# Where zeros for S are issued, and when the panels' lists are gathered, in a four-layer graph kernel

## The chip, the cores and the metric

The kernel runs on one core of one Trainium2 chip. The metric is the device time of one execution in microseconds (us); the time of a kernel is the median of its timed runs.

## The reference

Four graph layers are applied one after the other to `x` (32 batch entries, 512 nodes, 256 features, float32), with one adjacency matrix `adj` (512 x 512). An entry of `adj` is nonzero with probability of about 1.6%, and the diagonal always is.

```python
# layers 0 and 3 (h is x; own weights each)
pre_u, pre_v = h @ W1[:256], h @ W1[256:]
S   = sigmoid(relu(pre_u[:, :, None] + pre_v[:, None, :] + b1) @ W2 + b2)  # b, u, v
a_t = einsum('buv,bud->bvd', S * adj, h)
m_t = einsum('uv,bud->bvd', adj, h) * h
h   = beta1 * h + beta2 * (a_t @ Wa + ba) + beta3 * (m_t @ Wm + bm)
# layer 1
z   = h + relu((adj @ h) @ W + b)
# layer 2: attention over the nodes
feats = z @ W1.T ; f1 = feats @ W2 + b2
x   = softmax(leaky_relu(f1[:, None] + f1[None, :]) + adj) @ feats + bias2 + z
```

## The kernel before, in words

`S` is needed only where `adj` is nonzero. The kernel works it out for those places alone and puts the values into an array of zeros in HBM, which it then loads as a dense matrix. (If `adj` has too many nonzeros, another path computes S densely; it doesn't run with these inputs.)

**Groups.** The 32 batch entries go in 8 groups of 4 (`NB`). For each group `first` computes `pre_u` and `pre_v` of layer 0 and writes them to a `table` in HBM (`pre`, L574 to L582; a tile `puv` of 3 buffers, 256 KB for each write by SyncE). One row of the table holds one node's values for the 4 entries (4 KB). `edges` computes S from the table, `middle` does the rest of layer 0, layers 1 and 2, and writes the table of layer 3; `edges` runs again for layer 3, and `last` finishes.

**Items.** `edges` works on 36 items for each group (`ITEMS`). An item is a list of 128 edges, one for each partition. Item (c, k) holds, for each of the 128 rows of chunk c of `adj`, its k-th nonzero off the diagonal (4 chunks, 8 items each, `OWN`). Four further items are the panels: they hold what rows with more than 8 nonzeros have left. For each item GpSimd gathers 128 rows of the table by an index tile `iv` (`fetch`, L607, into `rows` with 5 buffers), VectorE adds the rows of the other end, `mine` (L686), applies relu and W2 (L694 or L702), and the sums go through the sigmoid (L592 to L597), are multiplied by the values of `adj` (L636) and scattered by GpSimd into `cells` in HBM, 16 bytes for each edge (`put`, L601). Scatters to one half of the cells wait for each other. The diagonal, `self_s`, is written by SyncE (L631). Gathers run 3 items ahead, or 5 where spare buffers are named (`rows_more`), which take tiles of the middle stage that aren't in use yet.

**Cells.** There is one pair of cell arrays for layer 0 and one for layer 3, 2 MB an array. Each has to be zero before its first scatter and keeps its zeros afterwards, since the same places are written for each group. A tile `zero` (128 x 1024, filled once by GpSimd) is written to each pair in 8 transfers of 512 KB (`zeros`, L538), for layer 0 in `setup`, for layer 3 in `zeros_behind`, which is listed for a time inside the first group's middle stage. All 16 go through SyncE's queue.

**Building the lists.** `Edges.build` finds the edges, once, on the chip. For each chunk a matmul counts nonzeros along each row (L310, L311); these ranks, with the row of `adj` beside them, are written to `lists` in HBM (L312, 4 transfers of 512 KB). `full` (L313, GpSimd) counts which rows are used up by a panel's line. Then, for the chunks in the order 0, 2, 1, 3, VectorE picks the values of the 8 items (L325) and ScalarE counts their columns (L336), and `slots` makes `iv` and `cell` (L387 to L396). After the four chunks come the panels: small matmuls and VectorE operations give the row of `adj` that each line of a panel belongs to (`node`, `inode`, `iu`; L347 to L362), four gathers bring these rows' lists (`got`, L368, GpSimd), and two VectorE operations for each (L374, L377) pick value and column.

**What sets the order.** Every stage is a generator. `sparse_path` lists the stages with due times in units of one group's middle stage, and `weave` takes their pieces in the order of these times. Each engine's order is then made by a scheduler that may take an instruction ahead of others if nothing keeps it back. `behind` gives an instruction an order (not a wait) after an instruction of a recent piece of the middle stage on its own engine, so that it isn't taken ahead of it. Transfers of zeros had no such order. A queue is worked through in order: an instruction that waits holds up those behind it on its engine. In the built program GpSimd's transfers take eight semaphores in turn, so each waits for the one eight before it.

Of the kernel before, what the change touches and what calls it, by code (L numbers as in the profile page):

```python
# [219 lines left out]
class Edges:  # L220
# [28 lines left out]
    def build(self, counts, adjT, lists, psum, big, tmp):  # L249

        nc, m = self.nc, self.m
        n_small = 1024

        def sheet(n):
            nonlocal n_small
            t = fl[:, n_small : n_small + n]
            n_small += n
            return t

        bf, fl = big(BF16, 4096), big(F32, 2048)  # L260
        upto = bf[:, 0 : NC * N].rearrange("p (c v) -> p c v", c=NC)
        nc.gpsimd.memset(upto, 1.0)
        nc.gpsimd.affine_select(upto, upto, [[-P, NC], [1, N]], ALU.is_ge, 0.0, 0, -1)
        maskT = bf[:, NC * N :].rearrange("p (c v) -> p c v", c=NC)
        before = fl[:, 0:P]
        nc.gpsimd.memset(before, 1.0)
        nc.gpsimd.affine_select(before, before, [[1, P]], ALU.is_gt, 0.0, 0, -1)
        line = fl[:, P : P + LINES]
        nc.gpsimd.iota(line, [[1, LINES]], 0, 0, allow_small_or_imprecise_dtypes=True)
        off = fl[:, 384:512]  # L270
        nc.vector.tensor_scalar(off, m.ident, -1.0, 1.0, ALU.mult, ALU.add)
        ones = fl[:, 512 : 512 + N]
        nc.vector.memset(ones, 1.0)
        step, halfstep = sheet(OWN), sheet(OWN)
        nc.gpsimd.iota(step, [[1, OWN]], 1, 0, allow_small_or_imprecise_dtypes=True)
        nc.vector.tensor_scalar(halfstep, step, -0.5, None, ALU.add)
        row = sheet(NC)
        nc.gpsimd.iota(row, [[0, 2], [P, 2]], 0, 1, allow_small_or_imprecise_dtypes=True)
        nc.vector.tensor_scalar(row, row, float(N), None, ALU.mult)
        spare = sheet(NC * OWN)  # L280
        nc.gpsimd.iota(
            spare, [[0, 2], [OWN * P, 2], [P, OWN]], CELLS, 1, allow_small_or_imprecise_dtypes=True
        )
        rows = []
        for _ in range(2):
            rows.append(big(F32, 2048).rearrange("p (c a v) -> p c a v", c=2, a=2))
        rows = [rows[c // 2][:, c % 2] for c in range(NC)]
        pb = psum()[:, 0:NC]
        base, end = sheet(NC), sheet(NC)
        for c in range(NC):  # L290
            cs, at = slice(c * P, (c + 1) * P), slice(c, c + 1)
            pt = m.adj_turned(c, psum)
            nc.vector.tensor_scalar(maskT[:, c, :], pt, 0.0, None, ALU.not_equal)
            nc.vector.tensor_tensor(maskT[:, c, cs], maskT[:, c, cs], off, ALU.mult)
            nc.scalar.copy(adjT[:, c, :], pt)
            pairs = [(before, counts.lines[:, at])]
            if c % 2:
                pairs.append((ones[:, 0:P], counts.lines[:, c - 1 : c]))
            mm(nc, pb[:, at], pairs)
            nc.gpsimd.tensor_copy(rows[c][:, 1, :], m.adj[:, c, :])  # L300
            nc.gpsimd.tensor_tensor(rows[c][:, 1, cs], rows[c][:, 1, cs], off, ALU.mult)
            yield
        nc.vector.tensor_scalar(base, pb, float(-OWN), None, ALU.add)
        nc.vector.tensor_tensor(end, pb, counts.lines, ALU.add)
        bf2 = big(BF16, 4096)
        full = bf2[:, 0 : NC * LINES].rearrange("p (c s) -> p c s", c=NC)
        for c in (0, 2, 1, 3):
            at = slice(c, c + 1)
            pr = psum()
            mm(nc, pr, [(maskT[:, r, c * P : (c + 1) * P], upto[:, r, :]) for r in range(NC)])  # L310
            nc.vector.tensor_scalar(rows[c][:, 0, :], pr, base[:, at], None, ALU.add)  # L311
            nc.sync.dma_start(lists[c * P : (c + 1) * P, :], rows[c].rearrange("p a v -> p (a v)"))  # L312
            nc.gpsimd.tensor_scalar(full[:, c, :], line, end[:, at], None, ALU.is_ge)  # L313
            yield
        acc, v, there, t = (sheet(NC * OWN) for _ in range(4))
        for c in (0, 2, 1, 3):
            at = slice(c, c + 1)
            js = slice(c * OWN, (c + 1) * OWN)
            target, bias = sheet(OWN), sheet(OWN)
            nc.vector.tensor_scalar(target, step, base[:, at], None, ALU.add)  # L320
            nc.vector.tensor_scalar(bias, halfstep, base[:, at], None, ALU.add)
            for k in range(OWN):
                j = slice(c * OWN + k, c * OWN + k + 1)
                junk = bf2[:, 2048 + k % 2 * N :][:, 0:N]
                nc.vector.scalar_tensor_tensor(  # L325
                    junk,
                    rows[c][:, 0, :],
                    target[:, k : k + 1],
                    rows[c][:, 1, :],
                    ALU.is_equal,  # L330
                    ALU.mult,
                    accum_out=self.value_of(c * OWN + k),
                )

                junk = bf2[:, 3072 + k % 2 * N :][:, 0:N]
                nc.scalar.activation(  # L336
                    junk, rows[c][:, 0, :], AF.Sign, bias=bias[:, k : k + 1], scale=-1.0, accum_out=acc[:, j]
                )
                if k % 2:
                    yield  # L340
            nc.vector.tensor_scalar(v[:, js], acc[:, js], 0.5, float(N // 2), ALU.mult, ALU.add)
            self.slots(js, v, there, t, row[:, at], spare)
            yield

        js = slice(NC * OWN, ITEMS)
        pu = psum()[:, 0 : 2 * PANELS]
        ones_bf = bf2[:, 1024:1025]  # L347
        nc.vector.memset(ones_bf, 1.0)
        for k in range(2 * PANELS):
            h, q = divmod(k, PANELS)  # L350
            mm(nc, pu[:, k : k + 1], [(full[:, h * 2 + c, q * P : (q + 1) * P], ones_bf) for c in range(2)])
        u, node, slot, start, sp, v, there, t = (sheet(2 * PANELS) for _ in range(8))
        nc.vector.tensor_scalar(u, pu, float(HALF - 1), None, ALU.min)
        nc.vector.tensor_copy(node, u)
        nc.vector.tensor_scalar(node[:, PANELS:], u[:, PANELS:], float(HALF), None, ALU.add)
        inode = self.inode
        nc.vector.tensor_copy(inode, node)
        nc.vector.tensor_scalar(self.iu, node, 2.0, None, ALU.mult)
        nc.gpsimd.iota(slot, [[0, 2], [P, PANELS]], 0, 1, allow_small_or_imprecise_dtypes=True)
        nc.vector.tensor_scalar(start, u, float(N), None, ALU.mult)  # L360
        nc.vector.tensor_scalar(sp, slot, float(CELLS + NC // 2 * OWN * P), None, ALU.add)
        nc.vector.tensor_scalar(t, slot, 1.0, None, ALU.add)  # L362
        yield
        gots = []
        for k in range(2 * PANELS):
            gots.append(tmp.tile([P, 2 * N], F32, name=f"got{k}", tag=("h1", "hT1", "mhT0", "hWa0")[k]))
            index = bass.IndirectOffsetOnAxis(ap=inode[:, k : k + 1], axis=0)
            nc.gpsimd.indirect_dma_start(out=gots[k], out_offset=None, in_=lists, in_offset=index)  # L368
        yield
        for k in range(2 * PANELS):  # L370
            at = slice(k, k + 1)
            rank, adj = gots[k][:, 0:N], gots[k][:, N:]
            junk = bf2[:, 2048 + k % 2 * N :][:, 0:N]
            nc.vector.scalar_tensor_tensor(  # L374
                junk, rank, t[:, at], adj, ALU.is_equal, ALU.mult, accum_out=self.value_of(NC * OWN + k)
            )
            nc.vector.scalar_tensor_tensor(junk, rank, slot[:, at], ones, ALU.is_le, ALU.mult, accum_out=v[:, at])  # L377
            yield
        self.slots(js, v, there, t, start, sp, 0)
        yield  # L380

    def slots(self, js, v, there, t, start, spare, off=None):
# [32 lines left out]
class Sparse:  # L415
# [25 lines left out]
    def psum(self):  # L441
        return self.ps.tile([P, N], F32, name="pst", tag="pst")
# [85 lines left out]
            yield  # L528

    def zeros_behind(self):  # L530
        self.zeros(self.cells["3"])
        yield

    def zeros(self, cells):
        for c in cells:
            flat = c[0:CELLS, :].rearrange("(q p a) b -> q p (a b)", q=4, p=P)
            for q in range(4):
                self.nc.sync.dma_start(flat[q], self.zero)  # L538

    def setup_behind(self):  # L540

# [537 lines left out]
def sparse_path(ctx, m, counts, xr, outr, B):  # L1079
# [10 lines left out]
    for t in range(last + 1):  # L1090
# [17 lines left out]
        if t == last:  # L1108
# [2 lines left out]
            behind = end + 0.29, end + 0.45  # L1111
        streams += [
            (sp.first(g0, t * NB), first, "fill"),
            (sp.edges(g0, ("yT", "mhT3") if t == 0 else ()), edges0, ""),
            (sp.middle(g0, g3, t * NB), spread(middle_shares(t == 0), start, end), "main"),
            (sp.edges(g3, ("yT", "h1", "hT1") if t == last else ()), edges3, "free"),
        ]
# [245 lines left out]
```

## Time and profile before

| | |
|---|---|
| timed runs, median of 3 | 3121.13 us (3118.4 to 3138.08) |
| the profiled execution, its own time | 3102.14 us |
| span of the profiled execution | 3100.4 us |
| granted TensorE clock, mean | 0.941 |
| PE, VectorE (DVE), ScalarE (ACT), GpSimd (POOL) busy | 2714.6, 2302.8, 1337.8, 1522.5 us |
| transfers | 679.40 MB, 219 GB/s over the span |
| `cells<-zero`: transfers, size, issue to landing (median) | 16 of 512 KB, 7.3 us |
| `got<-lists`: transfers, issue to landing (median) | 4, 6.2 us |
| `rows<-table`: gathers, issue to landing (median) | 554, 6.1 us |
| `cells<-self_s`: transfers, issue to landing (median) | 32, 6.1 us |

How to read it: the span runs from the first to the last instruction of one profiled execution. Times within it are us from its start. Busy times are averages over stages with different limits; the start, in which the lists are built and nothing of the middle stage can run, has other limits than the rest. In a timeline a row is one or several like instructions of one engine; SPq and POOLq mark the issue of a transfer by SyncE and GpSimd, and "POOL DMA_INDIRECT" is the issue of a gather or scatter.

### The profile page before, as it was taken

Reading aid. Unit: us, or ns where it says so; the run is one execution under the profiler, and the core shown is the slowest. Engines: PE = TensorE matmul, PEld = TensorE weight load, DVE = VectorE, ACT = ScalarE, POOL = GpSimd, SP = SyncE. Lnnn points to the kernel's source line nnn. Section 1 sums busy time; section 2 is a strip of 40 time slices with the busy share of each in tenths; the row PEclk is TensorE's granted clock in tenths of the full one; section 3 lists DMA queues with packets and bytes.
Section 4 is the critical chain, followed back from the end, with each engine's and each line's share of the span. In section 5 each row is a group of like instructions: output and inputs, shape, how many; then the busy total and the mean of one; then the engine's idle time right before and its main releaser. Section 6 shows DMA issues by size and latency. Waiting matters only on the chain.

```text
span 3100.4 us, 32465 instructions
## 1 busy us (share of the span) xinstructions
PE 2714.6 (88%) x8645; PEld 1642.5 (53%) x8646; DVE 2302.8 (74%) x6026; ACT 1337.8 (43%) x4101; POOL 1522.5 (49%) x1312
## 2 busy tenths in 40 slices
PE   6366888889998999989998999989999899889957
PEld 3133444446654565546664565545664566545636
DVE  6783886889589875989589885888679795772761
ACT  3453554445345433545354442545335343453440
POOL 1462453556346563556346562565436563450561
PEclk9688988999999999999999999999999999999978
DMA  8874556786677766786668766787568766551753
GB/s 285 282 236 152 180 174 225 237 268 213 223 224 263 235 210 219 247 282 213 227 213 258 238 197 213 242 267 237 188 216 268 251 221 208 178 174 58 234 195 115
DMA packets 302719, 679.40 MB, mean 219 GB/s; under 512 B 52672, under 2 KB 170944, under 8 KB 294336
## 3 DMA queue, kind: packets, MB, share of 16 engines
q0 software_dynamic: 120384, 406.01, 41.0%
q1 hardware_dynamic: 163184, 234.01, 22.5%
q10 hardware_dynamic: 18960, 37.24, 3.2%
q8 instruction: 70, 1.15, 0.2%
q14 instruction: 121, 0.99, 0.1%
HBM read 531.12 MB, written 146.01 MB: 218 GB/s over the span
## 4 chain that ended last, share of the span: by engine, by line
PE 51%; DVE 18%; DMA 17%; issue 6%; ACT 4%; POOL 3%; SPq 0%; POOLq 0%; ACTq 0%; DVEq 0%
PE pst L45 24%; PE pst L1001 7%; DVE rows L686 6%; DMA table<-puv 5%; DMA rows<-table,iv 5%; PE pst L570 3%; DVE rows L702 3%; PE pst L861 3%; PE pst L1010 3%; PE pst L572 3%; DMA cells<-s,cell 3%; DVE rows L694 3%; PE pst L883 2%; PE pst L840 2%; DMA SA<-cells 2%
## 5 line engine op out<-in xcount | busy, mean ns | idle before, releaser
L601 POOL DMA_INDIRECT cells<-s,cell x576 | 691.1, 1200 | 740.7 <-DMA cells<-s,cell 370.3
L607 POOL DMA_INDIRECT rows<-table,iv x554 | 663.3, 1197 | 672.7 <-DMA table<-puv 148.1
L686 DVE TENSOR_TENSOR rows<-rows,mine 128x1024 f32<-128x1024 f32 x554 | 670.8, 1219 | 164.7 <-DMA rows<-table,iv 148.8
L672 ACT ACTIVATE rows<-rows 128x256 f32<-128x256 f32 x1096 | 442.9, 407 | 516.7 <-DVE rows L694 511.1
L45 PE MATMUL pst<-adj,h 128*128 128x512 f32 x1024 | 451.3, 592 | 0.3 <-PE pst L941 0.3
L702 DVE SCALAR_TENSOR_TENSOR rows<-rows,L_gnn_W2bc 128x256 f32<-128x256 f32 x1120 | 415.9, 419 | 1.8
L45 PE MATMUL pst<-L_gnn_Wa,hT 128*128 128x256 f32 x1024 | 264.3, 410 | 118.6 <-DMA hT<-xT 64.6
L694 DVE SCALAR_TENSOR_TENSOR rows<-rows,L_gnn_W2bc 128x1024 f32<-128x1024 f32 x274 | 332.3, 1216 | 0.3
L45 PEld LDWEIGHTS pst<-adj,h 128*128 128x128 f32 x1024 | 192.8, 190 | 222.4 <-issue 218.4
L45 PEld LDWEIGHTS pst<-L_gnn_Wa,hT 128*128 128x128 f32 x1024 | 207.7, 208 | 165.8 <-issue 53.1
L45 PE MATMUL pst<-eT,feats 128*128 128x512 f32 x512 | 231.5, 606 | 12.4 <-ACT eT L953 12.4
L45 PE MATMUL pst<-adjT,zW 128*128 128x512 f32 x512 | 227.8, 597 | 6.2 <-ACT zW L865 6.2
L1001 PEld LDWEIGHTS pst<-hWa,SA 128*128 128x128 f32 x896 | 213.7, 328 | 7.7 <-issue 4.5
L1001 PE MATMUL pst<-hWa,SA 128*128 128x256 f32 x896 | 216.8, 398 | 0.0
L861 PE MATMUL pst<-WT,hT 128*128 128x256 f32 x512 | 150.3, 459 | 75.9 <-DVE hT L848 75.9
L672 ACT ACTIVATION_READ_ACCUMULATOR rows<-rows 128x1 f32 x1096 | 206.7, 189 | 0.0
L809 ACT COPY flat<-SA 128x512 f32<-128x512 f32 x128 | 137.6, 1128 | 155.0 <-PE pst L45 60.1
L840 PE MATMUL pst<-flat,hWa 128*128 128x512 f32 x448 | 196.8, 592 | 0.0
L861 PEld LDWEIGHTS pst<-WT,hT 128*128 128x128 f32 x512 | 118.0, 235 | 114.9 <-DVE hT L848 88.1
L575 ACT COPY puv<-pst 128x256 f32<-128x256 f32 x256 | 93.7, 370 | 183.8 <-DVE puv L574 168.1
L574 DVE TENSOR_TENSOR puv<-pst,bc_L_gnn_b 128x256 f32<-128x256 f32 x256 | 105.0, 416 | 90.3 <-DMA table<-puv 53.8
L45 PEld LDWEIGHTS pst<-eT,feats 128*128 128x128 f32 x512 | 97.5, 193 | 127.5 <-issue 109.8
(170 smaller groups left out, 3979.3 us busy)
## 6 DMA issues: line engine op xcount, KB each, us to landing
table<-puv SPq DMA_DIRECT2D x256, 256.0 KB, 5.5
SA<-cells POOLq DMA_DIRECT2D x64, 1024.0 KB, 7.0
h<-in_x_dram SPq DMA_DIRECT2D x64, 512.0 KB, 6.4
mine<-table SPq DMA_DIRECT2D x64, 512.0 KB, 5.3
hT<-xT SPq DMA_DIRECT2D x36, 512.0 KB, 5.1
h<-x2s SPq DMA_DIRECT2D x36, 512.0 KB, 4.1
xT<-hT ACTq DMA_DIRECT2D x32, 512.0 KB, 5.5
x2T<-yT SPq DMA_DIRECT2D x32, 512.0 KB, 5.3
```

What stands on the lines that cost most here:

```text
L45: nc.tensor.matmul(out, lhsT, rhs, start=(n == 0), stop=(n == len(pairs) - 1))
L574: nc.vector.tensor_tensor(puv[:, 0, :], pp[:, 0:D], w["b1bc"], ALU.add)
L601: self.nc.gpsimd.indirect_dma_start(out=g.cells[half], out_offset=bass.IndirectOffsetOnAxis(ap=at, axis=0), in_=s, in_offset=None)
L607: self.nc.gpsimd.indirect_dma_start(out=rows, out_offset=None, in_=g.table, in_offset=bass.IndirectOffsetOnAxis(ap=at, axis=0))
L672: self.behind(nc.scalar.activation(part, part, AF.Identity, accum_out=g.s[:, k, b : b + 1]))
L686: self.behind(nc.vector.tensor_tensor(rows, rows, other, ALU.add))
L694: nc.vector.scalar_tensor_tensor(by_entry, by_entry, 0.0, w2, ALU.max, ALU.mult)
L702: nc.vector.scalar_tensor_tensor(part, part, 0.0, w["W2bc"], ALU.max, ALU.mult, accum_out=at)
L809: self.nc.scalar.copy(flat[:, r, :], SA[r][:, :, b])
L840: nc.tensor.matmul(pz, hWa[:, r, cs], flat[:, r, :], start=(r == 0), stop=False)
L861: nc.tensor.matmul(pw[:, at], zT[:, d, cs], m.WT_1[:, d, :], start=(d + k == 0), stop=(d * k == 1))
L1001: nc.tensor.matmul(pz[:, k * D : (k + 1) * D], SA[r][:, cs, b], hWa[:, r, :], start=(r + k == 0), stop=False)
```

## The change

Three things are changed; everything else stays.

1. In `build`, the block that makes `node` and its like and gathers the panels' lists moves from after the four chunks to the middle of their loop, ahead of the third chunk (c = 1). The lists are gathered into other tiles: one tile for two of them with the tag `eT`, and those with the tags `h1` and `hT1`, where before it was `h1`, `hT1`, `mhT0` and `hWa0`. The operations that use the lists (L374, L377) stay at the end. The first group's `edges` takes `yT`, `mhT0` and `hWa0` as spare row buffers, where it took `yT` and `mhT3`.
2. `zeros` issues its 8 transfers from GpSimd's queue.
3. `zeros_behind` fills the tile `zero` again, with a VectorE memset that is ordered behind the middle stage. The zeros of layer 3 read that tile, so they wait for the memset.

```diff
         for c in (0, 2, 1, 3):
+            if c == 1:
+                pu = psum()[:, 0 : 2 * PANELS]
...
+                yield
+                gots = []
+                two = tmp.tile([P, 2, 2 * N], F32, name="got", tag="eT")
+                for k in range(2 * PANELS):
+                    if k < 2:
+                        gots.append(two[:, k, :])
+                    else:
+                        gots.append(tmp.tile([P, 2 * N], F32, name=f"got{k}", tag=("h1", "hT1")[k - 2]))
+                    index = bass.IndirectOffsetOnAxis(ap=inode[:, k : k + 1], axis=0)
+                    nc.gpsimd.indirect_dma_start(out=gots[k], out_offset=None, in_=lists, in_offset=index)
+                yield
             at = slice(c, c + 1)
...
-        gots = []
-        for k in range(2 * PANELS):
-            gots.append(tmp.tile([P, 2 * N], F32, name=f"got{k}", tag=("h1", "hT1", "mhT0", "hWa0")[k]))
-            index = bass.IndirectOffsetOnAxis(ap=inode[:, k : k + 1], axis=0)
-            nc.gpsimd.indirect_dma_start(out=gots[k], out_offset=None, in_=lists, in_offset=index)
-        yield
         for k in range(2 * PANELS):
...
     def zeros_behind(self):
+        self.behind(self.nc.vector.memset(self.zero, 0.0))
         self.zeros(self.cells["3"])
         yield
...
             for q in range(4):
-                self.nc.sync.dma_start(flat[q], self.zero)
+                self.nc.gpsimd.dma_start(flat[q], self.zero)
...
-            (sp.edges(g0, ("yT", "mhT3") if t == 0 else ()), edges0, ""),
+            (sp.edges(g0, ("yT", "mhT0", "hWa0") if t == 0 else ()), edges0, ""),
```

As built, GpSimd's order becomes: the eight zeros of layer 0, then the four L313; the first `got`, four gathers of `rows`, the other three `got`, four more gathers, and from there gathers and scatters as before. The eight zeros of layer 3 stand in the first group's middle stage, after the twelfth gather for the second group and ahead of that group's first scatter; their memset stands on VectorE between the L596 and L597 of that group's first four items.

More of the change, by code (lines that the diff above doesn't have):

```diff
@@ L316, in build @@
         for c in (0, 2, 1, 3):
+            if c == 1:
+                pu = psum()[:, 0 : 2 * PANELS]
+                ones_bf = bf2[:, 1024:1025]
+                nc.vector.memset(ones_bf, 1.0)
+                for k in range(2 * PANELS):
+                    h, q = divmod(k, PANELS)
+                    mm(nc, pu[:, k : k + 1], [(full[:, h * 2 + c, q * P : (q + 1) * P], ones_bf) for c in range(2)])
+                u, node, slot, start, sp, vp, therep, tp = (sheet(2 * PANELS) for _ in range(8))
+                nc.vector.tensor_scalar(u, pu, float(HALF - 1), None, ALU.min)
+                nc.vector.tensor_copy(node, u)
+                nc.vector.tensor_scalar(node[:, PANELS:], u[:, PANELS:], float(HALF), None, ALU.add)
+                inode = self.inode
+                nc.vector.tensor_copy(inode, node)
+                nc.vector.tensor_scalar(self.iu, node, 2.0, None, ALU.mult)
+                nc.gpsimd.iota(slot, [[0, 2], [P, PANELS]], 0, 1, allow_small_or_imprecise_dtypes=True)
+                nc.vector.tensor_scalar(start, u, float(N), None, ALU.mult)
+                nc.vector.tensor_scalar(sp, slot, float(CELLS + NC // 2 * OWN * P), None, ALU.add)
+                nc.vector.tensor_scalar(tp, slot, 1.0, None, ALU.add)
+                yield
+                gots = []
+                two = tmp.tile([P, 2, 2 * N], F32, name="got", tag="eT")
+                for k in range(2 * PANELS):
+                    if k < 2:
[5 more added lines that the diff above has]
+                yield
             at = slice(c, c + 1)
@@ L343, in build @@
             yield
[L345 to L348, printed above, removed]
-        for k in range(2 * PANELS):
[L350 to L362, printed above, removed]
-        yield
-        gots = []
-        for k in range(2 * PANELS):
-            gots.append(tmp.tile([P, 2 * N], F32, name=f"got{k}", tag=("h1", "hT1", "mhT0", "hWa0")[k]))
-            index = bass.IndirectOffsetOnAxis(ap=inode[:, k : k + 1], axis=0)
-            nc.gpsimd.indirect_dma_start(out=gots[k], out_offset=None, in_=lists, in_offset=index)
-        yield
         for k in range(2 * PANELS):
@@ L374, in build @@
             nc.vector.scalar_tensor_tensor(
-                junk, rank, t[:, at], adj, ALU.is_equal, ALU.mult, accum_out=self.value_of(NC * OWN + k)
+                junk, rank, tp[:, at], adj, ALU.is_equal, ALU.mult, accum_out=self.value_of(NC * OWN + k)
             )
-            nc.vector.scalar_tensor_tensor(junk, rank, slot[:, at], ones, ALU.is_le, ALU.mult, accum_out=v[:, at])
+            nc.vector.scalar_tensor_tensor(junk, rank, slot[:, at], ones, ALU.is_le, ALU.mult, accum_out=vp[:, at])
             yield
-        self.slots(js, v, there, t, start, sp, 0)
+        self.slots(slice(NC * OWN, ITEMS), vp, therep, tp, start, sp, 0)
         yield
```

## The prediction

> **What bounds the kernel now.** I read the page first, for the whole span.
>
> ```profile
> span 3100.4 us, 32465 instructions
> ...
> PE 2714.6 (88%) x8645; PEld 1642.5 (53%) x8646; DVE 2302.8 (74%) x6026; ACT 1337.8 (43%) x4101; POOL 1522.5 (49%) x1312
> ...
> DMA  8874556786677766786668766787568766551753
> ...
> PE 51%; DVE 18%; DMA 17%; issue 6%; ACT 4%; POOL 3%; SPq 0%; POOLq 0%; ACTq 0%; DVEq 0%
> ```
>
> Over the span TensorE is the bound, with VectorE in the chain. The first slices (77.5 us each) differ: the transfers are 8, 8 and 7 tenths busy there while PE stands at 6, 3, 6. On every engine the changed kernel's instructions stand in the same order as before from the second batch entry's softmax (355 us here) to the end, so what the change does is done in the first 360 us or so. There I read the chain of waits, then the queues.
>
> ```profile
> 38.14 7.20 DMA table<-puv
> ...
> 66.44 7.62 DMA table<-puv
> ...
> 78.62 4.52 DMA mine<-table
> ...
> 103.15 12.24 DMA cells<-self_s
> ...
> 138.15 4.26 DMA got<-lists,inode
> ...
> 268.22 7.49 PE pst L840 x10
> ```
>
> Start, duration, what: the chain of the start runs over transfers, and the middle stage's first sums (L840) begin at 268.2 us. SyncE's queue says why the transfers are late:
>
> ```profile
> 23.86 12.93 SPq L538 DMA_DIRECT2D cells<-zero  x8
> 38.14 0.61 SPq L582 DMA_DIRECT2D table<-puv  x1
> ...
> 87.20 3.95 SPq L538 DMA_DIRECT2D cells<-zero  x5
> 103.15 0.94 SPq L631 DMA_DIRECT2D cells<-self_s  x2
> ```
>
> The eight zero transfers of layer 0 hold SyncE for 12.9 us (1.6 us each; one `h` load takes 0.4), and the first `table` write and all `lists` writes stand behind them. The eight of layer 3, which nothing needs before the last stage, were pulled to 64.6 to 91.2 us: three between `table` writes, five just ahead of the diagonal `self_s`. Two waits and the transfers' rate complete it:
>
> ```profile
> POOL rows L607 <- DMA mine<-table: 52.8, 1, 52.8
> DVE big L374 <- DMA got<-lists,inode: 16.0, 1, 16.0
> ```
>
> ```profile
> 90.00:100.00 10.00, 1.86 (x8) 1.78 (x8) 8.85 (x10) 5.27 (x23) 4.52 (x4) 0.50 1.02 394
> 130.00:140.00 10.00, 0.00 (x0) 0.00 (x0) 0.00 (x0) 0.00 (x0) 6.46 (x7) 0.50 0.37 111
> ```
>
> Columns of the second: window, then busy us of PE, PE's loads, DVE, ACT, POOL, clock, share and GB/s of the transfers. At 90 us the transfers are full (394 GB/s); at 130 us everything but GpSimd stands still, because VectorE waits (126.5 to 142.4 us) for `got`, and `got` stands on GpSimd's queue behind scatters that wait for each other.
>
> **What the Trainium skill says.** "DMA: Bandwidth & Descriptors", section "Issuing engines are not separate DMA queues": transfers of SyncE, ScalarE and GpSimd run on the same 16 engines and interleave; another issuer saves issue time only. The trace agrees on the sharing: 364 to 401 GB/s from 30 to 50 us is one total. But here the issue time is the matter (12.9 us on SyncE). Same page, "Queues, rings and completion order": an engine takes turns between queues that have work, and takes each queue's descriptors in order. So zeros on GpSimd's queue no longer stand before `table`, but stand before any gather issued after them; no run here shows the turns. "SBUF — State Buffer", section "SBUF: two separate sides": some VectorE operations lock GpSimd out of writing descriptors. The gathers' 0.94 to 2.0 us fit that, without proving it.
>
> **The change, part by part.** Durations are of the profiled execution: span 3100.4 us, 3102.14 us with what lies around it; the three timed runs have a median of 3121.13, 19 us more, so I work out a difference and take it off the median.
>
> (a) Zeros of layer 0 leave SyncE. Eight issues go before GpSimd's four L313; GpSimd's plain transfers take about 0.58 us each (the two L727 at 262.1 take 1.15), so 5 us, and L313 (26.2 to 30.3 us) ends near 33. Its user, the four small matmuls for `node`, comes well after 40 us: nothing. The 4.19 MB still move. Gained: the stalls of VectorE and ScalarE behind `table` (4.5 us at 41, 3.3 us at 70), the `h` load that PE awaits for 6.2 us at 44, and ScalarE's 6.5 us at 28.7, spent in its own issues. These overlap. Two bounds: VectorE is busy 48.8 us between 20 us and its first gathered rows, so the first gather can't start before about 71; and 20 to 83 us move some 21.7 MB, less 1.6 MB for three zeros of layer 3, which at 380 GB/s take 53 us, so 73. I take 74 for 83.1: **-9 us** (-5 to -13).
>
> (b) Zeros of layer 3 leave the start. From the first gather, the first rows reach VectorE after 6.9 us (90.0); I take the median landing of 6.1, so 80. VectorE then works 13 us, nearly without a gap, to `self_s` (103.15), so 93. `self_s` landed after 12.2 us, behind 2.6 MB of zeros; the median of its 32 transfers is 6.1, so 99 instead of 115.4. That is 16 us in all, **-7** of them here (-3 to -10).
>
> (c) The lists' gathers leave the scatters. In the built order the first `got` stands ahead of the first gathered rows, three more after four rows, where GpSimd would soon wait for free buffers. The 16 us that VectorE waits are not all won: from 143 to 225 us GpSimd issues one transfer after another with gaps of 0.3 us, so GpSimd sets the rate, and what leaves its path is four issues of 0.96 us with gaps of 0.3: **-5 us** (-16 if VectorE sets the rate). Late next: the first scatters to one half, which wait for each other (116.2, 122.4, 126.5, 131.7); they stay. The third spare row buffer lets one more gather go early; nothing to a microsecond. VectorE has less time per item before the first scatter: it had worked 26 us from its first row by then, and would have 20, so I give back **+2** (0 to 5). `h1` and `hT1`, which hold the last two lists, come free with the last panel, as before.
>
> The start's sum: -9 - 7 - 5 + 2 = **-19 us** at L840.
>
> (d) Zeros of layer 3 in the middle stage. A new memset on VectorE (0.95 us, by GpSimd's own at 13.5 us) stands between L596 and the reciprocal at 330.1 us, and the eight transfers wait for it, on GpSimd, right after the gather at 329.3:
>
> ```profile
> 329.30 1.68 POOL L607 DMA_INDIRECT rows<-table,iv  x1 [0.84 <-DVE rows L702]
> 331.29 1.00 POOL L601 DMA_INDIRECT cells<-s,cell  x1 [0.30 <-issue]
> 332.59 0.95 POOL L607 DMA_INDIRECT rows<-table,iv  x1 [0.30 <-issue]
> ...
> 344.25 1.22 DVE L686 TENSOR_TENSOR rows<-rows,mine 128x1024 f32<-128x1024 f32 x1
> ```
>
> Behind them are the scatter of 331.3 and the gather of 332.6, whose rows VectorE takes at 344.25 (counted by buffers). Eight issues of 0.58 us move them to 336 and 337.3, and 4.19 MB go first: 10.5 us at 400 GB/s, 15 at 285. The rows then land at about 347 (to 352), VectorE is due at 345.2 with the memset, so it waits 2 us (0 to 8), and TensorE after it, since this is the softmax stretch whose chain is on VectorE and ScalarE. The scatters, each waiting for the one before, fall 13 us behind; GpSimd's idle 6 us at 355 and 9 us at 372 take that up, and their results are read at 457. Price: 0.95 + 2, rounded up for the next rows: **+4 us** (+1 to +9).
>
> Sum: -19 + 4 = **-15 us**: 3106 us, and about 3087 for a profiled execution.
>
> **Rivals.** *The wait goes whole* (0.15): VectorE, not GpSimd, sets the rate after 126 us, so its 16 us count (11 more), and (a) reaches its bound of 13 (4 more): -30, so 3091. For it: PE, DVE and ACT are all idle from 130 to 140. Against: GpSimd's unbroken issues after.
> *The start is bound by its bytes* (0.17): layer 0's zeros take a share of full transfers wherever they come from, so (a) is -3, (b) -4, (c) -5, +2, and (d) +4: -6, so 3115. For it: 364 to 401 GB/s from 30 to 50. Against: SyncE's 12.9 us with `table` waiting.
> *Slower* (0.10): the zeros clog GpSimd's queue at 331 us. If they get half of the page's mean of 219 GB/s, 4.19 MB take 38 us instead of 12, the rows for 344 us land near 372, VectorE and TensorE wait some 27 us, and 19 won become 8 lost: 3129. It decides once the zeros need more than about 31 us, that is under 135 GB/s. For it: gathers and scatters share that one queue (q0 is 41% of the transfers' time). Against: 394 GB/s were reached at 90 us by nearly the same mix.
>
> **How the numbers follow.** My forecast has 0.58, its own range is -25 to -5: 3096 to 3116. To leave no more than 2 in 10 out, the range reaches to the rivals, 3088 to 3126. A measurement of this kernel can tell about 1% (31 us) from no change. Faster by that needs the whole-wait rival and a little more, or the forecast's own bounds: 0.14. Slower needs the clog at well over its price: 0.05. The rest, 0.81, lies within.
>
> **What would show it.** Right: the first gathered rows are issued near 74 us, `self_s` lands near 99, `got` is waited for less than 2 us, L840 starts near 249 and VectorE waits 2 to 4 us some 14 us after the memset. (a) is wrong if the first gather is still past 79; (b) if `self_s` takes over 9 us; (c) if L840 is earlier by 16 us more than the landing of `self_s` is; (d) if no wait for rows follows the memset, or one over 10 us. The whole is wrong if L840 is less than 8 us or more than 30 us earlier.

## The result, and the profile after

| | before | after |
|---|---|---|
| median | 3129.84 us | 3117.05 us |
| lowest to highest | 3116.01 to 3138.08 us | 3106.34 to 3141.21 us |
| ratio, 95% interval | | 0.9966 (0.9954 to 0.9979) |

By the ratio the change saves 10.6 us of 3130 (6.6 to 14.4 by the interval; the two medians are 12.8 apart). Timed a second time the ratio was 0.9975 (0.9960 to 0.9991), 7.8 us. The forecast was 15 us off a median of 3121.13, 3106 us. That median came from the first three of the twenty runs of before that are in this table, so the ratio is the better measure. The kernel became faster, as forecast, by 0.7 and 0.5 of the 15 us in the two timings. But the gain is put together otherwise than was forecast: the zeros brought little, and the lists more (see below).

The page of the profile after, its span and busy times:

```profile
span 3112.8 us, 32475 instructions
...
PE 2713.5 (87%) x8645; PEld 1639.7 (53%) x8646; DVE 2302.9 (74%) x6027; ACT 1337.7 (43%) x4101; POOL 1531.2 (49%) x1328
```

This span is 12 us longer than that of before although the kernel is faster. So the two spans can't be subtracted: single executions of one kernel lie some 35 us apart, and both profiled executions of the kernel before (there is a second below) lie at the low end of its times. What can be read are marks early in the span, where the change works, and only beside their own scatter. The chain of waits of the profile after reaches back over the last few per cent of the span alone, so the start is read from the timeline. SyncE's queue first:

```profile
29.06 0.60 SPq L587 DMA_DIRECT2D table<-puv  x1
...
42.48 2.30 SPq L587 DMA_DIRECT2D table<-puv  x2
...
103.30 0.91 SPq L636 DMA_DIRECT2D cells<-self_s  x2
```

The 12.9 us of zeros are gone and the first `table` write is out at 29.06 in place of 38.14. But the second one is not out before 42.48 (it was 39.99). What SyncE waited for between them stands in its waits (first line: us in total, times, longest), and why it was late in the list of transfers from 20 to 60 us (count, size, median us from issue to landing):

```profile
SPq L587 <- DMA L_gnn_Wa<-in_L_gnn_Wa_dram: 9.4, 1, 9.4
```

```profile
cells<-zero POOLq DMA_DIRECT2D x8, 512.0 KB, 11.9
...
L_gnn_Wa<-in_L_gnn_Wa_dram ACTq DMA_DIRECT2D x1, 256.0 KB, 12.8
```

SyncE's and ScalarE's transfers share eight semaphores in the built program. A weight load of 256 KB that ScalarE issued at 29.55 landed only after 12.8 us, among GpSimd's zeros, and SyncE's next write had to wait for it. So SyncE is still held up, now between two `table` writes. GpSimd's timeline:

```profile
22.91 4.40 POOL L543 DMA_DIRECT2D cells<-zero  x8
...
75.36 1.36 POOL L345 DMA_INDIRECT got<-lists,inode  x1 [44.19 <-DVE inode L330]
80.00 0.98 POOL L612 DMA_INDIRECT rows<-table,iv  x1 [3.27 <-issue]
...
111.85 1.01 POOL L606 DMA_INDIRECT cells<-s,cell  x1 [11.80 <-DVE rows_more L691]
```

First gathered rows at 80.00 (83.13 before), first scatter at 111.85 (116.20). In the windows of before, VectorE had 0.00 us busy from 130 to 140; now:

```profile
90.00:100.00 10.00, 0.39 (x2) 0.39 (x3) 9.58 (x15) 6.12 (x29) 8.28 (x6) 0.50 1.03 411
...
130.00:140.00 10.00, 0.00 (x0) 0.00 (x0) 10.00 (x24) 4.45 (x21) 8.17 (x7) 0.50 0.67 189
```

VectorE is busy for nearly the whole of both windows, and `got` is no longer in its list of waits. TensorE's second burst of first sums, and then the middle stage, on GpSimd and on VectorE:

```profile
255.15 6.06 PE L845 MATMUL pst<-flat,big 128*128 128x512 f32 x10 [12.58 <-ACT flat L814]
```

```profile
317.30 4.32 POOL L543 DMA_DIRECT2D cells<-zero  x8 [0.63 <-DVE s L602]
```

```profile
316.09 0.91 DVE L535 MEMSET zero<- 128x1024 f32 x1 [0.15 <-issue]
...
334.16 1.22 DVE L691 TENSOR_TENSOR rows<-rows,mine 128x1024 f32<-128x1024 f32 x1 [3.31 <-DMA rows<-table,iv]
```

The sums start 13.1 us earlier than in the profile of before. Eighteen us after the memset VectorE has waited 3.3 us for rows, which were gathered behind the zeros.

### The profile page after: what moved, and what is told of

The parts are those of the page before. It is cut to its first block, busy times and chain, and to the rows that moved or that the text cites. A ratio compares the mean times of both kernels' runs of the same rounds, so it can differ in the third digit from the quotient of the medians.

```text
span 3112.8 us, 32475 instructions
## 1 busy us (share of the span) xinstructions
PE 2713.5 (87%) x8645; PEld 1639.7 (53%) x8646; DVE 2302.9 (74%) x6027; ACT 1337.7 (43%) x4101; POOL 1531.2 (49%) x1328
## 5 line engine op out<-in xcount | busy, mean ns | idle before, releaser
L866 PEld LDWEIGHTS pst<-WT,hT 128*128 128x128 f32 x512 | 121.4, 242 | 136.6 <-DVE hT L853 107.1
L579 DVE TENSOR_TENSOR puv<-pst,bc_L_gnn_b 128x256 f32<-128x256 f32 x256 | 104.4, 414 | 95.8 <-DMA table<-puv 58.6
```

The costliest lines, as they stand in the source:

```text
L579: nc.vector.tensor_tensor(puv[:, 0, :], pp[:, 0:D], w["b1bc"], ALU.add)
L866: nc.tensor.matmul(pw[:, at], zT[:, d, cs], m.WT_1[:, d, :], start=(d + k == 0), stop=(d * k == 1))
```

## The experiments

All times below are marks of one profiled execution each, in us from the start of its span, beside the timed ratio to the kernel before. "Sums" is the start of the second burst of first sums, "2nd" and "4th" are the second and fourth store of `x2T` by SyncE, that is, two points further on in the first group's middle stage.

| kernel | first rows | first scatter | sums | 2nd | 4th | ratio (95%) |
|---|---|---|---|---|---|---|
| before | 83.1 | 116.2 | 268.2 | 369.4 | 478.4 | |
| before_again | 80.6 | 111.9 | 266.0 | 366.2 | 472.3 | |
| after | 80.0 | 111.9 | 255.2 | 359.9 | 468.4 | 0.9966 (0.9954 to 0.9979) |
| after_again | 78.5 | 111.7 | 261.1 | 365.6 | 475.3 | 0.9975 (0.9960 to 0.9991) |
| lists_only | 81.9 | 109.0 | 255.1 | 355.9 | 465.1 | 0.9945 (0.9922 to 0.9969) |
| lists_only_2 | 80.6 | 105.7 | 254.3 | 353.5 | 462.6 | 0.9952 (0.9938 to 0.9966) |
| zeros_only | 79.0 | 112.8 | 265.6 | 370.2 | 478.2 | 0.9987 (0.9971 to 1.0003) |
| zeros3_early | 86.4 | 118.8 | 262.7 | 362.3 | 467.4 | 1.0003 (0.9984 to 1.0022) |
| zeros3_spread | 77.8 | 109.5 | 253.3 | 354.7 | 463.9 | 0.9956 (0.9941 to 0.9970) |
| zeros3_sync | 79.4 | 110.5 | 254.9 | 361.8 | 471.2 | 0.9972 (0.9957 to 0.9987) |
| zeros0_late | 77.6 | 111.1 | 255.4 | 362.6 | 468.7 | 0.9953 (0.9939 to 0.9968) |
| lists_spread | 81.5 | 107.4 | 255.6 | 359.8 | 466.0 | 0.9948 (0.9933 to 0.9964) |
| late_spread | 77.9 | 111.3 | 255.5 | 358.1 | 463.2 | 0.9965 (0.9944 to 0.9986) |
| more_gathers | 82.6 | 113.6 | 264.9 | 369.8 | 478.4 | 0.9986 (0.9970 to 1.0002) |
| zeros_more | 90.8 | 124.4 | 270.0 | 375.6 | 485.3 | 0.9994 (0.9979 to 1.0009) |

**The two kernels once more** (no edit).

> The changed kernel once more, for its marks in a second profile: first gathered rows issued at 80, first scatter at 112, the middle stage's first sums (second burst) at 255, fourth store of x2T at 468 us (before: 83, 116, 268, 478), and some 0.3% (10 us) under the kernel before. If the profile of before was only a lucky execution in its later part, the marks up to 500 us come again within 2 us and the span of this profile differs freely.

> The kernel before once more, for the scatter of its marks: first gathered rows 83, first scatter 116, first sums 268, fourth x2T store 478 us. If the first profile was a lucky execution only in its later part, these come within 3 us, and from the eighth to the sixteenth store takes some 710 us as in the other kernels' profiles, where the first profile had 700.

Of one and the same program the marks came up to 6 us apart (sums of the changed kernel 255.2 and 261.1, fourth store 478.4 and 472.3 before), so the 2 and 3 us of the expectations were too tight, and only means or differences over several kernels say something below 5 us. On means: first rows 81.9 before and 79.3 after, first scatter 114.1 and 111.8, sums 267.1 and 258.1, 2nd store 367.8 and 362.7. The stretch from the eighth to the sixteenth store took 700 and 702 us in the two profiles of before, and 706 to 717 in all others. In the built program nothing differs there and the timed runs say the opposite, so I put it down to these executions, without having shown what makes it.

**Each part alone.** `lists_only` takes the lists' part and leaves the zeros as before; `zeros_only` the reverse:

```diff
 lists_only (against after)
-        self.behind(self.nc.vector.memset(self.zero, 0.0))
         self.zeros(self.cells["3"])
...
-                self.nc.gpsimd.dma_start(flat[q], self.zero)
+                self.nc.sync.dma_start(flat[q], self.zero)
 zeros_only (against before)
+        self.behind(self.nc.vector.memset(self.zero, 0.0))
         self.zeros(self.cells["3"])
...
-                self.nc.sync.dma_start(flat[q], self.zero)
+                self.nc.gpsimd.dma_start(flat[q], self.zero)
```

> Only the lists' part of the change; all zeros stay on SyncE, without the memset. If the early lists carry the gain (theory): VectorE no longer waits for `got`, the first sums start some 9 us earlier than before (259), nothing is lost in the middle stage, so the fourth x2T store is near 469 and the time 8 to 10 us under before: as good as the whole change. If the zeros carry it (rival): first sums 263 to 264, the fourth store near 474, 4 us under before. If the parts only work together (rival): no change.

> Only the zeros' part: all on GpSimd's queue, those of layer 3 behind the memset; the lists are gathered late as before. Theory: first gathered rows near 80, first scatter near 112, but the wait for `got` of some 16 us is there, so the first sums come 3 to 5 us earlier than before (264) and the zeros in the middle stage take 5 us back: fourth store at 478, time equal to before within 3 us. Rival (the zeros carry the gain): first sums near 259, fourth store at 474, 5 us or more under before.

> The early lists alone, a second time, since the first was timed in seven runs only. If it is better than the whole change by what its zeros cost in the middle stage (about 4 us), it is again 14 to 18 us under before, ratio 0.9945 to 0.9955; first sums at 253 to 258, first sums to second x2T store 100 to 102. If the first was luck: 0.9965 to 0.9975 like the whole change.

The lists alone are worth 15 to 17 us, more than expected (8 to 10), and the zeros alone 4 (-1 to 9). The lists carry the gain, and with the zeros added it is smaller by the ratios (0.9966 and 0.9975), though the intervals overlap. SyncE's queue with the lists alone suggests why the zeros of layer 3, five of them behind the first gathers, hurt little there:

```profile
81.70 1.38 SPq L635 DMA_DIRECT2D cells<-self_s  x2
...
100.34 13.07 SPq L542 DMA_DIRECT2D cells<-zero  x5
```

In this program's order `self_s` stands 21 us earlier than in the changed kernel (103.30), ahead of the five zeros. So it isn't late for the first scatter, and the five zeros go out from 100 to 113 us, where VectorE waits for no transfer. The edit changes the built order as well as the queue, so what sets this kernel apart from the changed one isn't the price of the zeros alone. With the zeros alone, VectorE's wait for the lists is there, 10.7 us long.

**What the lists' gathers cost where they stood.** Four gathers of the same number of rows are put back on GpSimd into the scatter stretch, and nobody waits for them:

```diff
+        more = tmp.tile([P, 2 * N], F32, name="more", tag="mhT3")
+        quarters = lists.rearrange("n (a v) -> (n a) v", a=4)
+        for k in range(2 * PANELS):
+            index = bass.IndirectOffsetOnAxis(ap=self.iv[:, 3 * OWN + k : 3 * OWN + k + 1], axis=0)
+            out = more[:, k * N // 2 : (k + 1) * N // 2]
+            nc.gpsimd.indirect_dma_start(out=out, out_offset=None, in_=quarters, in_offset=index)
```

> The changed kernel with four more gathers of 128 rows on GpSimd in the scatter stretch, about where the lists' gathers stood before (after some eight scatters); their data, a quarter as wide, go into a tile that nothing reads. They put back the issue time that the change took off GpSimd's path there, 4 x 0.96 us and four gaps of 0.3, 5 us, and no wait of VectorE. If GpSimd sets the rate of that stretch (the step of the prediction), the first sums come 5 us later than with the changed kernel: 260 against 255 in the first profile, 266 against 261 in the second. If VectorE sets it (theory, after the lists alone gained 13 us there), 0 to 2 us later, and the time stays 0.2 to 0.4% under before.

```profile
143.56 1.14 POOL L379 DMA_INDIRECT more<-lists,iv  x1 [0.30 <-issue]
145.00 1.83 POOL L379 DMA_INDIRECT more<-lists,iv  x1 [0.30 <-issue]
147.14 1.51 POOL L379 DMA_INDIRECT more<-lists,iv  x1 [0.30 <-issue]
148.95 0.95 POOL L379 DMA_INDIRECT more<-lists,iv  x1 [0.30 <-DMA more<-lists,iv]
150.21 1.37 POOL L618 DMA_INDIRECT rows<-table,iv  x1 [0.30 <-ACT puv L586]
```

Here the theory that I had written down (VectorE sets the rate) fell and the step of the prediction stood. From the first scatter to the sums it takes 152.0, 154.0 and 152.8 us in the three profiles with late lists (mean 152.9) and 143.3 to 149.3 in the eleven with early lists and no extra gathers (mean 145.6). The four extra gathers, 6.65 us of GpSimd from 143.56 to 150.21, bring it to 151.3: 5.7 of the 7.3 us are back, though VectorE waits for nothing there (10.00 of 10 us busy in each window from 110 to 150). This is one profile, and the eleven spread over 6 us, so the 5.7 is known to some 2 us; the time agrees (0.9986 against 0.9966 and 0.9975). So GpSimd's issues lie on the path of the scatters. They aren't all of it: in the kernel before GpSimd also waits for earlier scatters to land, between 105 and 250 us:

```profile
POOL cells L601 <- DMA cells<-s,cell: 18.7, 9, 5.0
```

VectorE's wait for `got` was mostly slack, not the price: it was 16.0, 13.6 and 10.7 us in the three profiles with late lists, and the stretch of 152 to 154 us doesn't follow it. The third spare row buffer, which belongs to the lists' part, wasn't tried apart.

**The zeros of layer 3.** `zeros3_early` leaves them on SyncE without the memset (in the built order all eight then stand ahead of `self_s`); `zeros3_sync` sends them from SyncE behind the memset; `zeros3_spread` one at a time from GpSimd:

```diff
 zeros3_spread (against after)
         self.behind(self.nc.vector.memset(self.zero, 0.0))
-        self.zeros(self.cells["3"])
-        yield
+        for c in self.cells["3"]:
+            flat = c[0:CELLS, :].rearrange("(q p a) b -> q p (a b)", q=4, p=P)
+            for q in range(4):
+                self.behind(self.nc.gpsimd.dma_start(flat[q], self.zero))
+                yield
...
-        (sp.zeros_behind(), spread(even(2), 0.15, 0.2), ""),
+        (sp.zeros_behind(), spread(even(9), 0.15, 0.45), ""),
```

> The changed kernel, but layer 3's eight zeros stay on SyncE without the memset; in the built order all eight stand ahead of self_s. Theory: self_s lands later again (12 us or more), the first scatter is at 115 to 117 and the first sums near 259 to 260; in the middle stage VectorE's wait of 3.3 us for rows and the memset are gone, so the fourth store is near 468 to 470, the same as with the whole change: moving these zeros gained as much in the start as it cost later. Rival (the wait in the middle is hidden): the fourth store is at 473 or later. Rival (their bytes in the start cost nothing): first sums at 255 and the fourth store near 463.

> The changed kernel, but layer 3's eight zeros go out of SyncE's queue, still behind the memset, and stand after the second group's self_s there. If only the order on GpSimd's queue sets the price, first sums to second x2T store is 101 to 102. If bytes and a held queue count wherever they are (theory), the rows are late again or layer 3's table writes stand behind the zeros on SyncE: 103 to 106.

> The changed kernel, but layer 3's eight zeros are issued one at a time between the gathers and scatters of the middle stage, all behind the memset. So far the way from the first sums to the second x2T store took 104.5 to 104.7 us in the three profiles with the eight zeros in one block there, and 99.6 to 101.2 in the three without. Theory (the price is the rows standing behind 4 MB on GpSimd's queue): 101 to 102, VectorE's 3 us wait for rows gone, 2 to 3 us better than the whole change in total. Rival (the price is the bytes, or the memset's place): 104 to 105 as before, and nothing won.

From the sums to the 2nd store the five profiles without zeros in that stretch took 101.2, 100.3, 100.8, 99.2 and 99.6 (mean 100.2). With the block of eight on GpSimd it took 104.5 to 104.9 in four profiles and 105.6 and 107.1 in two: the block costs 4.4 us in the changed kernel and 5 over all. Spread, it took 101.4 here (102.6 and 104.2 in the two kernels below), about half, and VectorE's wait for rows is gone from its list. From SyncE it took 106.9, no better; VectorE waits as long for its rows, and the load of `mine` at 327.4 us stands behind the eight on SyncE:

```profile
DVE rows L691 <- DMA rows<-table,iv: 4.5, 1, 4.5
```

So the price is not a matter of GpSimd's queue alone: in these two kernels 4 MB in one go delay the rows from either queue. In the start the eight cost more (`zeros3_early`): first rows at 86.4 against 79.3 with the changed kernel, and 1.0003 in time, so nothing of the lists' gain is left. The expectation that moving them gains as much as it costs is refuted by the timing; its marks from the sums on (262.7, fourth store 467.4) would have fitted it. Where this kernel loses its time after the fourth store isn't shown.

**Layer 0's zeros later.** They wait for chunk 0's columns:

```diff
-        self.zeros(self.cells["0"])
         yield
-        for _ in range(NC + 2 * (OWN // 2 + 1)):
+        for k in range(NC + 2 * (OWN // 2 + 1)):
             next(edges)
+            if k == NC + OWN // 2:
+                self.nc.gpsimd.tensor_scalar(self.zero[:, 0:1], self.e.found, 0.0, None, ALU.mult)
+                self.zeros(self.cells["0"])
             yield
```

(`found` is the first column of `v`, as chunk 0's `slots` leaves it.)

> The changed kernel, but layer 0's zeros wait on GpSimd for the columns of chunk 0 (about 57 us, by a small operation of 128x1 that GpSimd puts ahead of them) in place of going out at 23 us. Theory (the start up to 60 us is bound by its bytes, so it did not matter which queue sent them): weights, lists and table land earlier, the first gathered rows are issued at 73 to 76 (changed kernel: 80.0 and 78.5), and the first sums come 3 to 5 us earlier. Rival (VectorE's work ahead of the index of the panels sets the first gather): 78 to 80 as before. Rival (the zeros now meet the lists and the first rows): first gather before 77 but first rows late by as much, no gain at the first sums.

Windows of this kernel, columns as above (the third busy time is VectorE):

```profile
30.00:40.00 10.00, 10.00 (x36) 4.90 (x35) 9.44 (x31) 3.48 (x10) 0.00 (x0) 1.00 0.92 325
40.00:50.00 10.00, 8.68 (x27) 4.27 (x26) 8.30 (x34) 7.84 (x22) 2.51 (x4) 1.00 1.02 359
50.00:60.00 10.00, 6.92 (x19) 2.72 (x18) 4.80 (x18) 5.02 (x14) 2.63 (x6) 0.84 1.03 404
60.00:70.00 10.00, 8.73 (x24) 3.99 (x25) 5.68 (x26) 2.54 (x7) 0.00 (x0) 0.65 0.92 332
```

From 30 to 50 us VectorE works 17.7 of 20 us where the changed kernel has 11.3 (6.23 and 5.05), and from 50 to 70, after the zeros went out at 48.1, only 10.5 where that has 18.1. The stall went with the zeros, and the first rows still stand at 77.6, where the five profiles with the changed kernel's start have 77.8 to 82.6. SyncE's wait for ScalarE's weight load was down from 9.4 to 2.0 us here, so that wait by itself doesn't set the first gather. In time the kernel was 0.9953, a little better than the changed one, but the intervals overlap.

**More zeros.** Layer 3's zeros are sent once more from GpSimd in the start, after L313:

```diff
-        for _ in range(NC + 2 * (OWN // 2 + 1)):
+        for k in range(NC + 2 * (OWN // 2 + 1)):
             next(edges)
+            if k == NC - 1:
+                self.zeros(self.cells["3"])
             yield
```

> The changed kernel with eight more zero transfers (layer 3's cells, once more than needed) on GpSimd's queue in the start, right behind the four L313, where GpSimd has nothing else to do. No other engine issues anything for them and no instruction reads what they write before the stage much later, so what they cost is their 4.19 MB alone. If the stretch up to the first gather is bound by its bytes (theory: that is why it did not matter which queue layer 0's zeros came from), 4.19 MB at some 390 GB/s are 10.7 us, less what the emptier stretch from 60 to 80 us takes up (0.22 of 20 us, 4): the index of the panels and the first gathered rows come 6 to 11 us later, rows at 85 to 90. If VectorE's own work and the order on the engines bind it (rival), 0 to 2 us later.

```profile
89.21 1.33 POOL L345 DMA_INDIRECT got<-lists,inode  x1 [44.43 <-DMA table<-puv]
90.84 0.98 POOL L614 DMA_INDIRECT rows<-table,iv  x1 [0.30 <-issue]
```

First rows at 90.8: 11.6 us later than the mean of the changed kernel, the whole 4.19 MB at 361 GB/s and nothing taken up by the emptier stretch, as far as a mark that scatters by some 2 us tells. VectorE's waits for `table` from 28 to 92 us rose from 11.0 to 22.2. All 11 us arrive at the sums (270.0 against 258.1). So bytes sent while the transfers are full (410, 406 and 412 GB/s from 30 to 60 us here) count one for one. Those sent later don't: `lists_only` and its repeat send three zeros of layer 3, 1.6 MB, from 60.7 to 71.6 us, `lists_spread` below sends none before 300 us, and the first rows stand at 81.9, 80.6 and 81.5.

**Two combinations.** `lists_spread` is `zeros3_spread` with layer 0's zeros on SyncE; `late_spread` is `zeros0_late` with the zeros of layer 3 spread.

> The early lists, layer 0's zeros on SyncE as before, and layer 3's zeros one at a time in the middle stage from GpSimd behind the memset. In the built order self_s stands early on SyncE, as with the lists alone (there issued at 81.7 us, with the changed kernel at 103.3). Theory: first scatter at 105 to 109, first sums at 252 to 255, first sums to second store 101 to 102, fourth store at 463 to 466, 16 to 20 us under before: the best of all. Rival (five of layer 3's zeros stood behind self_s anyway and cost nothing): no better than the lists alone; worse by 1 to 3 us if the spread zeros still hold up rows.

> The changed kernel with both: layer 0's zeros held back until chunk 0's columns are found, and layer 3's zeros one at a time in the middle stage. Theory (their gains add): first rows to VectorE at 84 to 86, first sums at 252 to 255, 101 to 102 us from there to the second x2T store, fourth store at 462 to 466 and 0.5 to 0.6% under before, as good as the lists alone. Rival (both run into the same limit): no better than either by itself, 0.45%.

Neither is better than the lists alone: 0.9948 and 0.9965, and the gains do not add. The best versions are `lists_only` (0.9945 and 0.9952, median 3096.7 us in its longer timing against 3113.9 of before) and `lists_spread` (0.9948), which can't be told apart. Both beat the kernel before; the lists alone are also ahead of the changed kernel, by some 4 to 9 us by the ratios, though the intervals of their second timings overlap (0.9938 to 0.9966 and 0.9960 to 0.9991). A start without layer 0's zeros at all wasn't tried, since the cells would then hold no defined values.

## Why the prediction was right and wrong, step by step

**(a) Layer 0's zeros off SyncE: -9 forecast, -2.6 measured** (first rows, means of two profiles each; against 83.1 the first profile alone gives -3.1). Without the lists' part it is the same (`zeros_only`, 79.0), so the first `got` ahead of the rows doesn't hold them up. This step failed, and so did (b): they missed by 6 and 7 us. By the prediction's own sign, the first gather was past 79 in one profile and just under in the other. The small parts were right: eight issues took 4.4 us, and L313 ended at 31 at no cost. What failed first is the gain that was counted on, VectorE's stalls behind `table`. They didn't go, they grew (28 to 92 us, before and after; 6.7 and 10.5 in the second profiles):

```profile
DVE puv L574 <- DMA table<-puv: 7.8, 2, 4.5
DVE puv L579 <- DMA table<-puv: 11.0, 6, 4.9
```

What failed next is "two bounds, I take 74": VectorE's work (71) and the bytes (73) were set side by side as if the larger one held. (By the trace they were also too high: VectorE is busy 48.1 us from 20 to 83.1, and the transfers move 317 GB/s there, 20.0 MB and not 21.7; that gives 68 for either.) In the run they follow one another in part. The windows of the changed kernel, columns as above:

```profile
30.00:40.00 10.00, 5.92 (x24) 2.83 (x22) 6.23 (x20) 0.90 (x4) 1.18 (x3) 0.99 1.04 409
40.00:50.00 10.00, 9.44 (x17) 3.93 (x18) 5.05 (x17) 4.17 (x12) 0.00 (x0) 0.67 0.99 362
...
60.00:70.00 10.00, 8.88 (x28) 4.29 (x27) 9.44 (x42) 7.01 (x20) 0.00 (x0) 1.00 0.78 266
70.00:80.00 10.00, 9.37 (x39) 4.70 (x38) 8.89 (x36) 7.23 (x21) 1.36 (x1) 1.00 0.78 252
```

From 30 to 50 us, while the zeros fill the transfers, `table` writes and weight loads are late and VectorE works 11.3 of 20 us; from 60 to 80 it works 18.3 and the transfers aren't full. Before, it was 15.1 and 14.6. (The second profiles have 16.5 and 16.8 before, 11.5 and 18.7 after.) The change moved VectorE's stall forward and did not remove it. `zeros0_late` turns the two halves round and gains 2 us at most at that point; `zeros_more` adds bytes to the full stretch and pays for them in full. The rival "bound by its bytes" had -3 here, and its mechanism is what the runs show for the full stretch. The sentence of the Trainium skill that the prediction set aside here ("DMA: Bandwidth & Descriptors", "Issuing engines are not separate DMA queues": another issuer saves issue time only) fits the -2.6 us better. SyncE's waits of the kernel before, from 23 to 37.5 us, already say so:

```profile
SPq L538 <- DMA xT<-hT: 3.5, 1, 3.5
SPq L538 <- DMA bc_L_gnn_beta<-in_L_gnn_beta_dram: 2.2, 1, 2.2
SPq L538 <- DMA col_L_gnn_b<-in_L_gnn_b_dram: 1.7, 1, 1.7
SPq L538 <- DMA big<-in_L_gnn_ba_dram: 1.2, 1, 1.2
SPq L538 <- DMA L_gnn_Wm<-in_L_gnn_Wm_dram: 0.4, 1, 0.4
```

9.0 of the 12.9 us in which the zeros held SyncE were waits for other transfers to land, ScalarE's above all. I had taken them for issue time. When the zeros were gone, SyncE waited 9.4 us for a landing instead.

**(b) Layer 3's zeros out of the start: -7 forecast, nothing or next to it at the first scatter** (-2.3 in all there, where (a) alone makes -2.6). The landing was right: `self_s` took 7.7 us in place of 12.2, under the 9 of its sign. It was issued at 103.30 all the same, because the terms ahead of it were too small: rows came to VectorE 7.9 us after the first gather and not 6.1, and VectorE needed 15.5 us to `self_s` and not 13, with picks of chunk 3 and `puv` work between the items. So 111 and not 99. The lists' gathers, which now stand among those of the rows, aren't the reason: in `zeros_only`, without them, VectorE needed 18.8 us there (85.6 to 104.4).

**(c) The lists off the scatters' path: -5 + 2 = -3 forecast, -7.3 measured.** The mechanism is right and shown: GpSimd's issues are on the path, VectorE's 16 us are not what counts, and four issues put back cost 5.7 of the 7.3 us. The reading behind it was too neat: of GpSimd's gaps between 143 and 225 us seven are longer than 0.3 us, 11.6 us in all. The mis-sized term is the give-back of 2 for VectorE, of which nothing is seen. `got` is not waited for at all (the sign was under 2 us). The sign against (c), that the sums gain 16 us more than the landing of `self_s`, didn't come.

**(d) Layer 3's zeros in the middle: +4 forecast, +4.4 measured** in the changed kernel, 5 over all kernels with the block. The memset took 0.91 us (0.95), the wait came 18 us after it (14) and was 3.3 and 4.4 us (2, bounds 0 to 8). GpSimd's queue did not clog: the eight landed after 6.9 us in the median, where the slower rival needed some 31 us for all of them.

**The sum.** At the sums -19 was forecast; the two pairs of profiles give -13.1 and -4.9, on means -9.0. With (d) that leaves -4.6 at the 2nd store (-5.1 read off), while the timed runs say -10.6 and -7.8. The difference is within what these marks scatter; I can't say more on it. That the total came as near as it did is in part luck: the zeros' parts of the start missed by some 14 us, and the lists' part made up for 4 of them. The range of 3088 to 3126 and the 1% bound held.

## What to carry to other kernels

Where transfers are full first and an engine has to catch up afterwards, the bound by bytes and the bound by work overlap only in part; the larger one alone is too low a figure. Test it by sending more bytes that nobody reads: in the full stretch they counted one for one here, later not at all. The length of a wait is not what its removal is worth: put the instructions that were waited for back without the wait and see how much of the gain goes. And price each part of a change alone, since one part can pay for the other: here the lists alone gained 15 to 17 us and the whole change 8 to 11.

## What the runs showed of the hardware that was not expected

- Eight plain transfers of 512 KB held SyncE for 12.9 to 14.9 us in the start, in five profiles; in the first, 9.0 us of it were waits for ScalarE's and its own earlier transfers to land. GpSimd issued eight in 4.3 to 4.5 us, in the start and in the middle stage. But a second eight close behind (`zeros_more`) took GpSimd 13.7 us, from 30.9 to 44.6, each but the first waiting for one of the zeros ahead to land.
- Gathers of 128 rows of 1 KB took GpSimd 0.95 to 1.83 us to issue, as long as those of 128 rows of 4 KB (0.94 to 2.0).
- Two executions of one program were 6 us apart 255 us after their start, and single executions up to 35 us apart at the end.
